# Four graph layers on one core: one pool of slabs from the first sweep through attention, and another order of the third sweep

## The chip, the cores and the metric

The kernel runs on one NeuronCore of a Trainium2 chip. Its engines are TensorE (PE, matrix products; PEld is its weight load), VectorE (DVE), ScalarE (ACT), GpSimd (POOL) and SyncE (SP, which here only issues transfers). The metric is the device time of one execution in microseconds, the median over several runs; lower is better. The time before is 1585.27 us, the median of 3 runs (1582.21 to 1586.68).

## The reference

There are 4096 nodes with 64 features, `x`, and one dense-stored 4096 x 4096 matrix `adj` of edge weights (0 or 0.05 to 0.06). Four layers follow one another, each with a residual sum and a layer norm over the features:

```python
x = _layernorm(x + _L0_gnn_ref(x, adj, ...))        # Chebyshev terms
x = _layernorm(x + _L1_gnn_ref(x, adj, adj, ...))   # graph attention and two GRU cells
x = _layernorm(x + _L2_gnn_ref(x, adj, ...))        # sum over neighbours, weights decaying with rank
x = _layernorm(x + _L3_gnn_ref(x, adj, ...))        # hyperbolic aggregation
```

Layer 0 is what most of the change touches: with `T0 = x`, `T1 = adj @ x`, `T2 = 2 adj @ T1 - T0`, `T3 = 2 adj @ T2 - T1`, the sum of `Tk @ W[k]` over k. Layer 1 needs, for every node, the features summed over the positive entries of its row (a product with the mask `adj > 0`), the same for the negative ones, softmax weights that depend only on the sign of an entry, and the product of the row with the features. Both signs are provided for; these inputs hold none below zero.

## The kernel before, in words

`adj` is cut into 8 x 8 slabs (g, c) of 512 x 512, 1 MB each: row group g (four blocks of 128 rows) and chunk c (four blocks of 128 columns). PE contracts over partitions, so a slab has to stand transposed; the kernel transposes all of `adj` once, keeps the transposed slabs `at` in a DRAM scratch `adj_t`, and reads them from there later.

**First sweep** (lines 525 to 577). For every g and for c from 7 down, SP loads a slab as `raw` (line 169, pool `rows0` with five buffers of 8 KB per partition), PE transposes its 16 blocks (line 536), ACT copies them out (line 543), POOL's queue writes the slab to `adj_t` (line 567), DVE reduces `raw` twice: row sums (line 569) and the lowest entry (line 571). Slabs with c >= g at once serve for `T1`, those with c < g for both `T1` and the part of `T2` that can be had already; each row group ends in `after_first`. Beside it run the loads and small preparations of weights (`aside`) and the transposes of `x` into `tr_a` (line 519, through `to_columns`, line 201). Six slabs stay in SBUF (`here`: (7,0) to (7,3), (6,6), (7,7)).

**Second sweep** (lines 617 to 626): the slabs with c > g, from g = 6 down, finish `T2`. A group ends in `after_second`: ACT copies the sum (line 447), PE brings it back to rows by products with the identity (line 467), DVE stores `T2` (line 600), PE multiplies by the layer's weights (line 457) and DVE adds that to `acc_t` (line 602).

**Third sweep** (lines 633 to 645): the slabs with c <= g give `T3`; group g has g + 1 slabs. The groups come in the order 7, 0, 1, 2, 3, 4, 5, 6. PE runs eight half-width products per slab (line 436). A group ends in `after_third`, put off by one slab (`Behind`): ACT copies the sum (line 447), PE forms the product with the weights plus `acc_t` times the identity (line 467, sixteen instructions), DVE adds `x` (line 608), norms, centres and splits into three bf16 parts (lines 230 to 261, 215 to 219). The normed rows are turned into `tr_a` (`turned_third`, line 614, through line 201) after the next group's slabs; the last group's turn is left to attention. Slabs are read back through `load0` (line 591) into the buffers of `rows0`.

**Attention** (`attention`, lines 870 to 977) goes through all 64 slabs again, g from 7 down, c from 0 up. It stands in a branch on whether any entry is negative; code inside a branch isn't mixed with code outside it. `masks` loads a slab (`load1`, line 660), DVE forms the mask `pos` (line 665), POOL's queue writes it to `mask_t` for layer 2 (line 669), and PE runs `wide` (line 906), `narrow` (line 914) and `weighed` (line 923), about 3.1 us in all. Masks are made two slabs ahead (`lead`). Steps of the previous group's end (`group_end`) follow one by one after slabs. The slabs' buffers are four of the pool `cols1`, and one in `front`, which is loaded and masked ahead of the branch. Near the end, and wherever the planner finds SP free, the first masks of layer 2 are loaded (`load2`, lines 680 to 683).

Layer 2 (lines 1052 to 1126) and layer 3 (from line 1143) follow.

**What sets the order.** Instructions are written in program order and a planner orders each engine's queue by its own estimate of when operands are there, earlier code first; `in_order` holds chosen instructions in their written order among themselves. [...] Buffers of a pool are given in rotation. Pools are laid out one after another; a pool opened after another was closed can take its place, and its first writers then wait for the last readers of what was there. `tri` (lines 123 to 135), a helper for the constant `follow`, is such a short-lived pool ahead of `rows0`.

Of the kernel before, what the change touches and what calls it, by code (L numbers as in the profile page):

```python
# [9 lines left out]
F32 = mybir.dt.float32  # L10
# [50 lines left out]
def gnn4_kernel(  # L61
# [21 lines left out]
    nc = tc.nc  # L83
# [14 lines left out]


# [60 lines left out]
    def gcols(g):  # L160
        return slice(g * GW, (g + 1) * GW)


    first_p = ctx.enter_context(ExitStack())
    rows_p = first_p.enter_context(tc.tile_pool(name="rows0", bufs=5))

    def load_raw(g, c):
        raw = rows_p.tile([P, GB, CB * P], F32, name="raw", tag="raw")
        nc.sync.dma_start(raw, adj[gcols(g), c * CB * P : (c + 1) * CB * P].rearrange("(b p) j -> p b j", p=P))
        return raw  # L170

    first_raw = [load_raw(0, NCH - 1)]
# [227 lines left out]


# [5 lines left out]
    with first_p, tc.tile_pool(name="acc", bufs=1) as acc_p, tc.tile_pool(name="win", bufs=1) as win_p, tc.tile_pool(  # L407
# [64 lines left out]
        dpart = sm.tile([P, NG, NCH, GB], F32, name="dpart")  # L472
        lows = sm.tile([P, NG * NCH], F32, name="lows")
# [122 lines left out]
        def after_second(g, ps):  # L596
            gs = gblocks(g)
            t_v = out_of(ps, "t_v")
            o = times(new_post(), [(t_v, ident[:, 0:F])])
# [4 lines left out]
        def after_third(g, ps):  # L604
            gs = gblocks(g)
            o = times(new_post(), [(out_of(ps, "t_h"), cheb[:, 3, :]), (acc_t[:, g // 2, :], ident[:, mine(g)])])
# [26 lines left out]
        done = []  # L633
        for n, g in enumerate([NG - 1] + list(range(NG - 1))):
            ps = ps_a.tile([P, GW], F32, name="pass3", tag=("h_ps", "w_ps")[n % 2])
            for c in reversed(range(g + 1)):
                at = load0(g, c)
                for k in range(CB):
                    halves(ps, 2, at[:, k, :], c * CB + k, c == g and k < 2, c == 0 and k >= CB - 2)
                later.flush()  # L640
            while done:
                turned_third(done.pop())
            later.push(lambda g=g, ps=ps: [after_third(g, ps), done.append(g)])
        later.flush()
        not_turned = done.pop()
# [12 lines left out]
    def load1(pool, g, c):  # L658
        at = pool.tile([P, CB, GW], F32, name="at1", tag="at")
        nc.sync.dma_start(at, adj_t[g][:, c * CB : (c + 1) * CB, :])  # L660
        return at

    def positives(pool, at):
        pos = pool.tile([P, CB, GW], MASK, name="pos")
        in_order(nc.vector.tensor_scalar(pos, at, 0.0, None, ALU.is_gt, saturate=False))  # L665
        return pos

# [19 lines left out]

# [5 lines left out]
    front = ctx.enter_context(ExitStack())  # L693
    front_p = front.enter_context(tc.tile_pool(name="front", bufs=1))
    with_at = [load1(front_p, NG - 1, c) for c in range(1)]
    with_pos = [positives(front_p, at) for at in with_at]


# [171 lines left out]
    def attention(signed, cols_p, sg, tl, ps_a, ps_p):  # L870
# [3 lines left out]
        def masks(g, c):  # L874
            if g == NG - 1 and c < len(with_at):
                at, pos = with_at[c], with_pos[c]
            else:
                at, pos = load1(cols_p, g, c), None
# [17 lines left out]
            up = sg.tile([P, CB, GW], F32, name="up")  # L896
# [34 lines left out]
        else:  # L931
# [5 lines left out]
        lead = 1 if signed else 2  # L937
        ahead = [masks(*order[n]) for n in range(lead)]
        steps = [
            lambda ps_p: to_columns(  # L940
                ps_p, tr_a[0 : F + 1, gcols(not_turned)], nat_a[:, gblocks(not_turned), :], F + 1, nc.scalar.copy
            )
        ]
# [36 lines left out]
    for signed in (True, False):  # L980
        with tc.If(any_negative > 0) if signed else cmp.Else() as block:
            cmp = block
            with tc.tile_pool(name="cols1", bufs=4 if not signed else 2) as cols_p, tc.tile_pool(name="sign1", bufs=2 if signed else 5) as sg, tc.tile_pool(
# [4 lines left out]
                attention(signed, cols_p, sg, tl, ps_a, ps_p)  # L988
# [521 lines left out]
```

## Time and profile before

| what | value |
|---|---|
| median of 3 runs | 1585.27 us (1582.21 to 1586.68) |
| the profiled execution | 1581.82 us, of which its span 1580.0 us |
| first sweep, from its first transposes | 18 to 374 us |
| second sweep | 376 to 488 us |
| third sweep, to attention's first product | 488 to 604 us |
| attention | 604 to 889 us |
| layers 2 and 3 | 889 to 1108, 1108 to 1580 us |
| busy share: PE, DVE, ACT, POOL | 90%, 74%, 52%, 6% |
| adj slabs, us from issue to landing (median) | `raw` 12.1, `at` 5.2 |

The page gives busy shares, the span in 40 slices with busy tenths, TensorE's granted clock and the load of the transfer engines, and groups of instructions by line. Answers of the trace give the waits (who waited, for whom, total us, times, longest), and the instructions of an engine in order of time, with start and length; in brackets stands the idle time before one and what ended it. In a list of stretches each line holds start and end, length, busy time of PE, PEld, DVE, ACT and POOL with the number of their instructions, granted clock, transfer share and GB/s. `SPq` is SP's own queue. Idle time of an engine that nobody waits for costs nothing.

### The profile page before, as it was taken

The page shows a single profiled execution, that of the slowest core. Times are in us where ns is not written, and L with a number is a line of the kernel's source. Part 1 is how long each engine was busy: PE and PEld are TensorE (multiplying, and loading weights), DVE is VectorE, ACT ScalarE, POOL GpSimd, SP SyncE. Part 2 cuts the span into 40 slices and gives each one's busy share as a digit, 9 for nine tenths or more (in the row PEclk, how much of TensorE's full clock was granted, in tenths as well). Part 3 has the DMA queues.
Part 4 walks back from the last instruction along what each step waited for, and adds up shares of the span by engine and source line. Part 5 has one row for each costly group of instructions (what it writes and reads, how often), then busy time and mean ns, then how long its engine had stood idle before and what let it go on. Part 6 is the DMA issues. An engine that isn't in the chain of part 4 may idle for free.

```text
span 1580.0 us, 19139 instructions
## 1 busy us (share of the span) xinstructions
PE 1418.8 (90%) x6851; PEld 691.3 (44%) x6874; DVE 1166.3 (74%) x2268; ACT 820.1 (52%) x1367; POOL 96.7 (6%) x162
## 2 busy tenths in 40 slices
PE   6899999999998987989999998789789999899995
PEld 4555555554443432333434444445333434344343
DVE  6788988982001534665676688888899999999997
ACT  3444444431000100222222588779888999898895
POOL 3001101000000001111111100000000000000000
PEclk9899999999999998999999999999899999999998
DMA  8999999996776778878978654442425444434430
GB/s 300 409 378 390 413 412 400 379 354 229 249 279 243 265 294 317 300 277 290 333 288 299 201 173 157 137 131 84 182 85 194 153 180 170 163 139 179 162 115 13
DMA packets 102336, 383.81 MB, mean 243 GB/s; under 512 B 15828, under 2 KB 16856, under 8 KB 70232
## 3 DMA queue, kind: packets, MB, share of 16 engines
q1 hardware_dynamic: 84256, 296.78, 52.9%
q0 software_dynamic: 14592, 84.16, 13.0%
q10 hardware_dynamic: 3384, 1.56, 0.5%
q8 instruction: 57, 0.93, 0.2%
q14 instruction: 47, 0.39, 0.1%
HBM read 297.26 MB, written 85.20 MB: 242 GB/s over the span
## 4 chain that ended last, share of the span: by engine, by line
PE 28%; DVE 22%; ACT 6%; DMA 2%; issue 2%; ACTq 0%; DVEq 0%; SPq 0%
PE v_ps L1227 6%; DVE wt L1103 5%; PE sums_ps L1287 4%; PE a_ps L923 3%; PE cnt_ps L1095 3%; DVE rt L1445 2%; DVE at_m L1273 2%; PE acc_ps L1064 2%; DMA at<-adj_t 2%; PE p_ps L906 2%; DVE f L1430 2%; PE post L729 1%; DVE at_d L1433 1%; DVE pos L665 1%; PE post L1271 1%
## 5 line engine op out<-in xcount | busy, mean ns | idle before, releaser
L543 ACT COPY at<-tp 128x512 f32<-128x512 f32 x256 | 133.0, 598 | 151.4 <-issue 106.2
L1101 ACT ACTIVATE wt<-cnt_ps 64x512 uint16<-64x512 f32 x288 | 163.1, 587 | 27.7 <-PE cnt_ps L1095 23.2
L1103 DVE TENSOR_SCALAR wt<-cnt_ps 64x512 uint16<-64x512 f32 x224 | 151.5, 692 | 29.6 <-PE cnt_ps L1095 23.8
L1227 PE MATMUL v_ps<-rv,tr_a 128*128 128x512 f32 (+1 forms) x288 | 142.2, 618 | 33.4 <-DVE rt L1445 32.5
L1095 PE MATMUL cnt_ps<-m,follow 128*64 128x512 fp8e4 x480 | 136.3, 390 | 23.1 <-DVE wt L1103 10.7
L569 DVE TENSOR_REDUCE dpart<-raw 128x4 f32<-128x2048 f32 x64 | 145.4, 2271 | 9.8 <-DMA raw<-in_adj_dram 9.8
L571 DVE TENSOR_REDUCE lows<-raw 128x1 f32<-128x2048 f32 x64 | 145.2, 2269 | 0.0
L536 PE MATMUL tp<-ident,raw 128*128 128x128 f32 x1024 | 133.7, 285 | 8.6 <-DMA raw<-in_adj_dram 8.6
L1287 PE MATMUL sums_ps<-at_d,nat_c 128*64 128x512 f32 x288 | 139.8, 606 | 1.4 <-DVE at_d L1433 1.0
L536 PEld LDWEIGHTS tp<-ident,raw 128*128 128x128 f32 x1024 | 117.2, 146 | 50.2 <-issue 41.2
L923 PE MATMUL a_ps<-at,nat_a 128*64 128x512 f32 x512 | 124.5, 613 | 2.9 <-DVE at L889 2.9
L665 DVE TENSOR_SCALAR pos<-at 128x2048 fp8e4<-128x2048 f32 x72 | 87.0, 1221 | 53.3 <-DMA at<-adj_t 43.4
L1292 PE MATMUL sums_ps<-at_m,nat_c 128*64 128x512 f32 x224 | 108.2, 605 | 0.0
L443 PE MATMUL w_ps<-at,cheb_n 128*128 128x512 f32 x224 | 101.1, 595 | 0.0
L443 PE MATMUL pass<-at,cheb_n 128*128 128x512 f32 x224 | 98.3, 596 | 0.7 <-DVE cheb_n L594 0.7
L1064 PE MATMUL acc_ps<-wt,sup_two 128*64 128x512 bf16 x512 | 96.6, 391 | 0.0
L1227 PEld LDWEIGHTS v_ps<-rv,tr_a 128*128 128x128 f32 x288 | 53.0, 199 | 83.9 <-DVE rt L1445 40.7
L1456 ACT ACTIVATE rt<-rt,one_col 128x1024 f32<-128x1024 f32 x72 | 78.7, 1094 | 17.4 <-DVE rt L1445 17.2
L1445 DVE SCALAR_TENSOR_TENSOR rt<-v_ps,rt 128x1024 f32<-128x1024 f32 x72 | 83.2, 1157 | 3.8 <-ACT rt L1421 3.6
L1430 DVE SCALAR_TENSOR_TENSOR f<-rt,w 128x1024 f32<-128x1024 f32 x72 | 82.8, 1158 | 3.3 <-ACT rt L1456 3.3
L1433 DVE TENSOR_TENSOR at_d<-at_d,f 128x1024 f32<-128x1024 f32 x72 | 83.2, 1156 | 0.1
L1273 DVE TENSOR_TENSOR at_m<-post,at_m 128x512 f32<-128x512 f32 x112 | 74.9, 683 | 9.6 <-PE post L1271 9.1
(346 smaller groups left out, 2262.3 us busy)
## 6 DMA issues: line engine op xcount, KB each, us to landing
at<-adj_t SPq DMA_DIRECT2D x122, 1024.0 KB, 5.2
raw<-in_adj_dram SPq DMA_DIRECT2D x64, 1024.0 KB, 12.1
adj_t<-at POOLq DMA_DIRECT2D x64, 1024.0 KB, 8.2
at_d<-adj_t SPq DMA_DIRECT2D x36, 1024.0 KB, 4.8
at_m<-adj_t SPq DMA_DIRECT2D x28, 1024.0 KB, 6.9
mask_t<-pos POOLq DMA_DIRECT2D x64, 256.0 KB, 6.1
m<-mask_t SPq DMA_DIRECT2D x120, 128.0 KB, 2.8
m<-mask_t SPq DMA_DIRECT2D x60, 256.0 KB, 4.1
```

What stands on the lines that cost most here:

```text
L443: in_order(nc.tensor.matmul(ps, lhsT=cheb_n[:, jb, k : k + 2, :], rhs=rhs, start=first, stop=last))
L536: in_order(nc.tensor.transpose(tp[:, cols(b)], raw[:, b, cols(k)], ident))
L543: nc.scalar.copy(at[:, k, :], tp)
L569: in_order(nc.vector.tensor_reduce(dpart[:, g, c, :], raw, AX.X, ALU.add))
L571: in_order(nc.vector.tensor_reduce(lows[:, n : n + 1], raw.rearrange("p b j -> p (b j)"), AX.X, ALU.min))
L923: in_order(nc.tensor.matmul(ps[q * F : (q + 1) * F, :], lhsT=nat_a[:, c * CB + k, 0:F], rhs=parts[q if signed else 0][:, k, :], start=(c = ...
L1064: in_order(nc.tensor.matmul(acc[a][q * F : (q + 1) * F, :], lhsT=parts[part], rhs=wt[2 * a + q].bitcast(BF16), start=(jb == NB - 1 and par ...
L1095: in_order(nc.tensor.matmul(cnt[q][mine, :], lhsT=follow, rhs=chunks[c][odd][q][:, k, :], start=(h == 2 * NB - 1), stop=True, skip_group_c ...
L1101: in_order(nc.scalar.activation(w, cnt[q][mine, :], AF.Relu, scale=-128.0))
L1103: in_order(nc.vector.tensor_scalar(w, cnt[q][mine, :], -128.0, 0.0, ALU.mult, ALU.max))
L1227: nc.tensor.matmul(vs[n][:, k, cs], lhsT=tr_a[:, cols(jb)], rhs=rights[i][0][:, cs], start=True, stop=True)
L1287: in_order(nc.tensor.matmul(bank[0:F, :], lhsT=nat_c[:, j * CB + k, :], rhs=own[t][:, k, :], start=(i == j and k == 0), stop=(j == seq[-1] ...
```

## The change

It has five parts.

- The pool of slabs `rows0`, and a small pool `front`, are laid out first, on the other side of SBUF, and stay until attention is over. The first slab's load stands first in the program.
- `attention` takes its slabs from `rows0` (five buffers) in place of its own pool `cols1` (four). `load1` and `positives` move up.
- The second sweep's ends go back to rows by transposes in place of products with the identity. The third sweep's ends are cut in three: `third_weighed` multiplies by the weights on the wide side and adds into `acc_t`; `after_third` transposes that, adds `x`, norms and splits; `turned_third` turns as before.
- The third sweep's groups come as 7, 0, 6, 1, 5, 2, 4, 3, and the three steps of an end are due one, two and six slabs after the group's last slab.
- After the last slab, four slabs for attention are asked for and the first mask is formed; then what is left of the ends runs, the last group's turn with it.

`dpart` and `lows` move to a pool that the first layer closes, and `up`, which only the signed branch uses, to another pool.

```diff
--- before.py
+++ after.py
@@ -96,6 +96,21 @@
     sm = ctx.enter_context(tc.tile_pool(name="sm", bufs=2))
     dram = ctx.enter_context(tc.tile_pool(name="dram", bufs=1, space=DRAM))
+    def gcols(g):
+        return slice(g * GW, (g + 1) * GW)
+    front = ctx.enter_context(ExitStack())
+    rows_p = front.enter_context(tc.tile_pool(name="rows0", bufs=5, side="right"))
+    front_p = front.enter_context(tc.tile_pool(name="front", bufs=1, side="right"))
+    def load_raw(g, c):
+        raw = rows_p.tile([P, GB, CB * P], F32, name="raw", tag="raw")
+        nc.sync.dma_start(raw, adj[gcols(g), c * CB * P : (c + 1) * CB * P].rearrange("(b p) j -> p b j", p=P))
+        return raw
+    first_raw = [load_raw(0, NCH - 1)]
     ident = const.tile([P, P], F32, name="ident")
     make_identity(nc, ident)
@@ -157,19 +172,6 @@
     mask_t = [dram.tile([P, NB + 1, GW], MASK, name=f"mask_t{g}") for g in range(NG)]
     none_t = const.tile([HP, GW], MASK, name="none_t")
-    def gcols(g):
-        return slice(g * GW, (g + 1) * GW)
-    first_p = ctx.enter_context(ExitStack())
-    rows_p = first_p.enter_context(tc.tile_pool(name="rows0", bufs=5))
-    def load_raw(g, c):
-        raw = rows_p.tile([P, GB, CB * P], F32, name="raw", tag="raw")
-        nc.sync.dma_start(raw, adj[gcols(g), c * CB * P : (c + 1) * CB * P].rearrange("(b p) j -> p b j", p=P))
-        return raw
-    first_raw = [load_raw(0, NCH - 1)]
     nc.scalar.dma_start(nat_a[:, :, 0:F], x.rearrange("(b p) f -> p b f", p=P))
     nc.gpsimd.memset(nat_a[:, :, F : F + 1], 1.0)
@@ -398,13 +400,23 @@
             lambda: state("hhe", whh_e), lambda: state("hhn", whh_n), turned_gat, gat_and_cell, score_weights,
         ]
-    with first_p, tc.tile_pool(name="acc", bufs=1) as acc_p, tc.tile_pool(name="win", bufs=1) as win_p, tc.tile_pool(
+    def load1(g, c):
+        at = rows_p.tile([P, CB, GW], F32, name="at1", tag="raw")
+        nc.sync.dma_start(at, adj_t[g][:, c * CB : (c + 1) * CB, :])
+        return at
+    def positives(pool, at):
+        pos = pool.tile([P, CB, GW], MASK, name="pos")
+        in_order(nc.vector.tensor_scalar(pos, at, 0.0, None, ALU.is_gt, saturate=False))
+        return pos
+    with tc.tile_pool(name="acc", bufs=1) as acc_p, tc.tile_pool(name="win", bufs=1) as win_p, tc.tile_pool(
         name="cols0", bufs=4
     ) as cols_p, tc.tile_pool(name="diag0", bufs=2) as diag_p, tc.tile_pool(
         name="ps_t0", bufs=3, space=PSUM
@@ -469,8 +481,8 @@
                     )
             return o
-        dpart = sm.tile([P, NG, NCH, GB], F32, name="dpart")
-        lows = sm.tile([P, NG * NCH], F32, name="lows")
+        dpart = acc_p.tile([P, NG, NCH, GB], F32, name="dpart")
+        lows = acc_p.tile([P, NG * NCH], F32, name="lows")
         later = Behind(1)
         put_off = []
@@ -596,14 +608,22 @@
         def after_second(g, ps):
             gs = gblocks(g)
             t_v = out_of(ps, "t_v")
-            o = times(new_post(), [(t_v, ident[:, 0:F])])
+            o = new_post()
+            for b in range(GB):
+                nc.tensor.transpose(o[:, b, :], t_v[0:F, cols(b)], ident[0:F, 0:F])
             nc.vector.scalar_tensor_tensor(cheb_n[:, gs, 2, :], o, 2.0, part[:, gs, :], ALU.mult, ALU.add)
             o, to = weigh(g, [(t_v, cheb_23)])
             nc.vector.tensor_tensor(to, o, to, ALU.add)
-        def after_third(g, ps):
+        def third_weighed(g, ps):
+            o, y_t = weigh(g, [(out_of(ps, "t_h"), cheb[:, 3, :])])
+            nc.vector.tensor_tensor(y_t, o, y_t, ALU.add)
+        def after_third(g):
             gs = gblocks(g)
-            o = times(new_post(), [(out_of(ps, "t_h"), cheb[:, 3, :]), (acc_t[:, g // 2, :], ident[:, mine(g)])])
+            o = new_post()
+            for b in range(GB):
+                nc.tensor.transpose(o[:, b, :], acc_t[mine(g), g // 2, cols(b)], ident[mine(g), mine(g)])
             y = sm.tile([P, GB, F], F32, name="y0", tag="y")
             nc.vector.tensor_tensor(y, o, nat_a[:, gs, 0:F], ALU.add)
             layernorm(nat_a[:, gs, 0:F], y)
@@ -630,19 +650,28 @@
                 deg[:, gblocks(g)], dpart[:, g, :, :].rearrange("p c b -> p b c"), AX.X, ALU.add
             )
-        done = []
-        for n, g in enumerate([NG - 1] + list(range(NG - 1))):
-            ps = ps_a.tile([P, GW], F32, name="pass3", tag=("h_ps", "w_ps")[n % 2])
+        due, n = [], 0
+        for m, g in enumerate(sum(([NG - 1 - i, i] for i in range(NG // 2)), [])):
+            ps = ps_a.tile([P, GW], F32, name="pass3", tag=("h_ps", "w_ps")[m % 2])
             for c in reversed(range(g + 1)):
                 at = load0(g, c)
                 for k in range(CB):
                     halves(ps, 2, at[:, k, :], c * CB + k, c == g and k < 2, c == 0 and k >= CB - 2)
                 later.flush()
-            while done:
-                turned_third(done.pop())
-            later.push(lambda g=g, ps=ps: [after_third(g, ps), done.append(g)])
-        later.flush()
-        not_turned = done.pop()
+                while due and due[0][0] <= n:
+                    due.pop(0)[2]()
+                n += 1
+            due += [
+                (n, m, lambda g=g, ps=ps: third_weighed(g, ps)), (n + 1, m, lambda g=g: after_third(g)),
+                (n + 5, m, lambda g=g: turned_third(g)),
+            ]
+            due.sort(key=lambda d: d[:2])
+        with_at = [load1(NG - 1, c) for c in range(4)]
+        with_pos = [positives(front_p, with_at[0])]
+        for work in due:
+            work[2]()
     three = ctx.enter_context(tc.tile_pool(name="three", bufs=1))
@@ -655,16 +684,6 @@
     sup_two = late.tile([P, NB, 2 * F], BF16, name="sup_two")
     sup_lo = late.tile([P, NB, F], BF16, name="sup_lo")
-    def load1(pool, g, c):
-        at = pool.tile([P, CB, GW], F32, name="at1", tag="at")
-        nc.sync.dma_start(at, adj_t[g][:, c * CB : (c + 1) * CB, :])
-        return at
-    def positives(pool, at):
-        pos = pool.tile([P, CB, GW], MASK, name="pos")
-        in_order(nc.vector.tensor_scalar(pos, at, 0.0, None, ALU.is_gt, saturate=False))
-        return pos
     def keep_mask(mask, g, c):
         nc.gpsimd.dma_start(mask_t[g][:, c * CB : (c + 1) * CB, :], mask)
@@ -684,16 +703,11 @@
         return to[QG:], to[:QG]
     last_p = [late.tile([P, GW], F32, name=f"last_p{q}") for q in range(2)]
     last_a = late.tile([P, GW], F32, name="last_a")
     wq = late.tile([P, 2, H3], F32, name="wq")
     first_masks = [late.tile([P, CB, GW], MASK, name=f"first_mask{n}") for n in range(2 * QG)]
-    front = ctx.enter_context(ExitStack())
-    front_p = front.enter_context(tc.tile_pool(name="front", bufs=1))
-    with_at = [load1(front_p, NG - 1, c) for c in range(1)]
-    with_pos = [positives(front_p, at) for at in with_at]
@@ -867,15 +881,15 @@
         return [lambda ps_p, part=part: [work(ps_p) for step in part for work in step] for part in parts]
-    def attention(signed, cols_p, sg, tl, ps_a, ps_p):
+    def attention(signed, sg, tl, ps_a, ps_p):
         Q = 2 if signed else 1
         def masks(g, c):
             if g == NG - 1 and c < len(with_at):
-                at, pos = with_at[c], with_pos[c]
+                at, pos = with_at[c], with_pos[c] if c < len(with_pos) else None
             else:
-                at, pos = load1(cols_p, g, c), None
+                at, pos = load1(g, c), None
             if not signed and pos is None:
                 pos = positives(sg, at)
             mask = pos
@@ -893,7 +907,7 @@
             if not signed:
                 return (pos,), (at,)
             neg = sg.tile([P, CB, GW], MASK, name="neg")
-            up = sg.tile([P, CB, GW], F32, name="up")
+            up = tl.tile([P, CB, GW], F32, name="up")
             in_order(nc.vector.tensor_scalar(neg, at, 0.0, None, ALU.is_lt, saturate=False))
             nc.scalar.activation(up, at, AF.Relu)
             in_order(nc.vector.tensor_scalar_min(at, at, 0.0))
@@ -934,13 +948,9 @@
             nc.gpsimd.memset(wq[:, 1, :], 0.0)
             nc.gpsimd.memset(last_p[1], 0.0)
         order = [(g, c) for g in reversed(range(NG)) for c in range(NCH)]
-        lead = 1 if signed else 2
+        lead = 0 if signed else 2
         ahead = [masks(*order[n]) for n in range(lead)]
-        steps = [
-            lambda ps_p: to_columns(
-                ps_p, tr_a[0 : F + 1, gcols(not_turned)], nat_a[:, gblocks(not_turned), :], F + 1, nc.scalar.copy
-            )
-        ]
+        steps = []
         for n, (g, c) in enumerate(order):
             if n + lead < len(order):
                 ahead.append(masks(*order[n + lead]))
@@ -980,12 +990,12 @@
     for signed in (True, False):
         with tc.If(any_negative > 0) if signed else cmp.Else() as block:
             cmp = block
-            with tc.tile_pool(name="cols1", bufs=4 if not signed else 2) as cols_p, tc.tile_pool(name="sign1", bufs=2 if signed else 5) as sg, tc.tile_pool(
+            with tc.tile_pool(name="sign1", bufs=2 if signed else 5) as sg, tc.tile_pool(
                 name="tail1", bufs=1
             ) as tl, tc.tile_pool(name="ps_a1", bufs=1 if signed else 2, space=PSUM) as ps_a, tc.tile_pool(
                 name="ps_p1", bufs=2, space=PSUM
             ) as ps_p:
-                attention(signed, cols_p, sg, tl, ps_a, ps_p)
+                attention(signed, sg, tl, ps_a, ps_p)
     front.close()
     nc.gpsimd.memset(tr_o, 0.0)
```

## The prediction

> **What bounds the kernel now.** I read the page's slices first, then the waits of SP, then busy time by stretch, then PE's waits and its order of time in the third sweep, and last SP's waits in attention. Slices of 39.5 us:
>
> ```profile
> span 1580.0 us, 19139 instructions
> ...
> PE   6899999999998987989999998789789999899995
> ...
> PEclk9899999999999998999999999999899999999998
> ```
>
> Up to slice 16 PE is at nine tenths except in slices 0 and 1 (to 79 us) and 12, 14 and 15 (474 to 513, 553 to 632 us); the clock digit falls in 1 and 15. The change touches just these places; the later dips lie in attention and layers it leaves alone. The stretches below give busy time by engine, clock and DMA share:
>
> ```profile
> 18.00:138.00 120.00, 108.72 (x618) 66.40 (x619) 102.41 (x89) 55.88 (x113) 11.73 (x22) 0.94 1.02 392
> 138.00:338.00 200.00, 200.00 (x1037) 118.24 (x1036) 176.21 (x134) 87.72 (x171) 19.66 (x37) 1.00 1.02 396
> 376.00:488.00 112.00, 111.54 (x290) 50.14 (x290) 6.68 (x12) 4.45 (x8) 0.00 (x0) 1.00 0.73 253
> 488.00:604.00 116.00, 93.61 (x454) 41.38 (x455) 48.99 (x203) 11.83 (x25) 0.72 (x2) 0.91 0.70 258
> 604.00:889.00 285.00, 261.75 (x1256) 109.68 (x1257) 178.19 (x511) 59.61 (x124) 46.98 (x65) 0.98 0.82 294
> ```
>
> The first sweep (18 to 374) has PE and DMA both full, the second (376 to 488) is PE alone, the third (488 to 604) is neither: PE idles 22 us there and its clock is 0.91. Why the first sweep starts at 18 is in SP's waits up to 18 us:
>
> ```profile
> SPq L169 <- DVE follow L135: 11.4, 1, 11.4
> ```
>
> The first slab of the adjacency is issued at 12.23, when DVE has last read the small `tri` tile: the buffers of `rows0` lie where `tri` was. PE's waits from 488 to 604, SP's from 480 to 604, and PE's order of time:
>
> ```profile
> PE post L201 <- DVE nat_a L261: 12.2, 5, 4.6
> PE post L467 <- ACT t_h L447: 2.2, 3, 0.7
> ```
> ```profile
> SPq L660 <- PE post L467: 12.8, 1, 12.8
> ```
> ```profile
> 513.51 3.68 PE L436 MATMUL pass<-at,cheb_n 128*64 128x512 f32 x8
> ...
> 519.25 1.94 PE L436 MATMUL pass<-at,cheb_n 128*64 128x512 f32 x8
> ...
> 604.10 1.86 PE L906 MATMUL p_ps<-pos,sp_two 128*128 128x512 fp8e4 x4 [7.77 <-DVE pos L665]
> ```
>
> The turn of a normed row (L201) waits for its norm while slabs stand ready behind it; after such a wait eight matmuls take 3.68 us, not 1.94. The first mask comes 7.77 us after the sweep's last matmul: its slab was not asked for until then (SP's 12.8), and DVE had the last norm first. In attention, PE waits only 8.3 us for masks after the first, and SP is held by loads of already written masks:
>
> ```profile
> SPq L680 <- DMA mask_t<-pos: 30.5, 4, 13.2
> ```
>
> **What the Trainium skill says.** "TensorE: Matmul & The Clock Gate", What's actually happening: about 3.4 us of idleness halve the clock, about 3.4 us of work restore it. The trace agrees (3.68 against 1.94), though 2.78 us of waiting sufficed at 524. "DMA: Bandwidth & Descriptors", Queues, rings and completion order: a DMA engine takes turns between queues by packet. No trace here shows x against slabs. "Perfetto Trace Analysis", Transposes: use a transpose rather than a plain matmul with the identity. The trace agrees: such a matmul of fp32 is two instructions (L467, eight for four blocks, 1.04 us), a transpose one (L201, four in 0.58).
>
> **The change part by part.**
>
> *Layout and first load.* On the right side `rows0` shares nothing with `tri`, so the load leaves at about 0.8 instead of 12.23: at most 11.4 us. Three things take from that. Now x (issued 0.86, landed 8.5, alone then) shares the engines; with two slabs of 2.6 us each (1 MB at 406 GB/s) between its packets it lands near 13. ACT issues fourteen small loads until 11.9 and loads its table, so its first copy is at 12.8, the first eviction of a slab (19.16 before) about 13. And 23 of the 32 transposes of x (0.16 each, 3.7 us of PE) ran inside the wait and now meet a full PE. Against that, PE's 8.6 us of waits for slabs between 18 and 100 mostly go, as DMA is ahead. I take 6.5: the 6 us by which evictions come earlier, the last two terms nearly cancelling; ends 3 and 11. PE never waits for a slab after 100 us, so what is won stays. `dpart` and `lows` only move: nothing.
>
> *Second sweep's ends* turn by transposes: eight instructions at 1.04 us become four at about 0.52. PE is full, so 7 x 0.5 = 3.5 us (0.5 of it beside the third sweep's start). Ends 2 and 4.
>
> *Third sweep.* Before, 488.3 to 604.1 is 115.8 us: 36 slabs x 1.71 = 61.6; the last end of the second sweep 1.9; eight ends of sixteen L467 instructions, 2.13 each, 17.0; seven turns x 0.58 = 4.1; waits 12.2 + 2.2 + 0.7; the last 7.8. These make 107.5; the 8.3 left are the half clock.
> After: 61.6 + 1.9 + eight ends of weighing (two L457 instructions, 0.87), four transposes (0.52) and a turn (0.58), 15.8: 79.3. (The 0.5 above is already counted with the second sweep.) Work of a row's end is now due one, two and six slabs after it, and a long row follows each short one. From y to the centred row DVE needs 4.5 us (596.4 to 600.8), with its splits 6.2. The turn, at least four slabs (6.8 us) after its norm starts, is covered. What is late next is the sum in `acc_t`: it stands on DVE behind the neighbour row's norm, and the transposes wait for it. For rows 0, 1 and 2 the distance falls short by about 4.6, 2.9 and 1.2 us; a half clock follows the first two, some 4 us. Where DVE takes the sum in its gap for ACT's root, most of this goes. The planner may also advance an end, as at 565.92 now (2.78 us). I take 10 us for all; ends 3 and 20.
> Slabs: 30 less five loaded ahead, and the first of attention, 26 x 2.6 = 68 us, under PE's 79: not the bound, but close.
>
> *Seam.* Four slabs of attention are issued on SP in the sweep, ahead of the branch, each when PE frees a buffer; attention's later loads queue behind. The first mask (1.22 us of DVE) stands ahead of the last row's sum and norm. That adds a wait: should its slab be late, sum, norm and both turns of row 3 wait on DVE and PE. The slab lands about one slab time behind the sweep's last, so I count 1.9 us. The last turn, formerly behind attention's first slab, now stands before the branch and waits for the norm. So PE loses ACT's copy 0.75, 1.9, and the norm 4.7: 7.4 us, hardly less than the 7.8 of before.
> After in all: 79.3 + 10 + 7.4 = 96.7, a gain of 19; ends 7 and 27.
>
> *Attention.* Four buffers of `cols1` and one used once become five in rotation: one more slab (3.1 us of PE work) of lead while masks block SP. Of the 8.3 us of waits for masks I take 2; ends -4 and 6, as the planner orders the same loads anew. `up` concerns the signed branch, not run. PE's work, mask writes on POOL and the later stages stay.
>
> *Sum:* 6.5 + 3.5 + 19 + 2 = 31. The profiled execution took 1581.8 (span 1580.0 and 1.8 around it), 3.5 below the median of 1585.3. The gain leaves 1549 of the span, and 1554 of the median.
>
> **Rivals.**
> *Small gain:* the planner puts row ends ahead of slabs that are in fact there, and x starves behind five slabs at the start. For it: L201 stalls after three slabs of row 5 show that the planner's slabs come later than real ones. Against: the ends' work is shorter and due later. 3 + 3 + 8 + 1 = 15: 1570. That the layout does not free the first load belongs here too; it costs the 6.5.
> *Large gain:* no half clock inside the sweep and DMA's head start fully used: 11 + 3.5 + 26 + 4 = 44: 1541. For it: PE's eight slab waits and clock drops at 43, 64 and 108 us lie in the first sweep's start. Against: DMA share 1.02 and ACT's issuing.
> *Slower:* mask loads placed early on SP hold all slabs of attention behind them, now that SP is ahead. Four such blocks exist, the longest 13.2 us. Five buffers cover 5 x 3.1 = 15.5 us; losing the 31 gained and 5 more over four groups needs blocks of 15.5 + 9 = 24.5 us each. From there it decides; at 30 us, 4 x 14.5 = 58 lost: 1612. Against: a mask written is 6.1 us away from its landing, and the extra slab is the very cover.
>
> **How the numbers follow.** Forecast 0.55 (own range 1546 to 1563), small 0.22, large 0.14, slower 0.05; no change 0.04. The range, 1541 to 1575, cuts part of the outer cases. 0.3% (4.8 us) is about what a measurement of this kernel tells from no change. Faster 0.91, same 0.04, slower 0.05.
>
> **What would show it.** First slab issued before 2 us, first eviction near 13, second sweep begun 6 us earlier; half as many instructions in the second sweep's turns; no L201 wait over 1 us inside the third sweep, but waits of transposes on DVE's `acc_t`; attention's first matmul near 575 (604 - 6.5 - 3.5 - 19); the first mask's DVE instruction before the last norm. I am wrong if the first evictions stay at 19, if the third sweep waits on slabs, or if attention takes longer than its 285 us.

## The result

The changed kernel takes 1923.2 us (median of four, 1922.2 to 1923.6), the kernel before, timed beside it, 1583.8 (1582.2 to 1586.7). The ratio is 1.2139, with a 95% interval of 1.2118 to 1.2161: slower by 21%, where the forecast was 1554 and faster.

From here on, line numbers are those of the changed kernel, and "attention" is the stretch from its first to its last `wide` product (L920; L906 before). The expectations below count it to the end of its last products, some 3 us longer (284 where the table here has 281.1). The page of the changed kernel, with its head, slices of 48 us, the row of the mask instruction and the row of the slab load:

```profile
span 1920.5 us, 18940 instructions
...
PE   6999999999976646555555556798798899999995
...
PEclk9999999999997777777676767899898999999998
...
L410 DVE TENSOR_SCALAR pos<-at 128x2048 fp8e4<-128x2048 f32 x72 | 87.9, 1225 | 317.0 <-DMA at<-adj_t 316.6
...
at<-adj_t SPq DMA_DIRECT2D x122, 1024.0 KB, 4.8
```

From slice 12 (576 us onwards, counted from 0) to slice 25 PE falls to between four and seven tenths, and the digit of its clock to six or seven but for the last. The mask instruction's own work is what it was (87.9 us in 72), but DVE sat idle 317.0 us ahead of it, nearly all of that for slabs; before, 53.3, of which 43.4 for slabs:

```profile
L665 DVE TENSOR_SCALAR pos<-at 128x2048 fp8e4<-128x2048 f32 x72 | 87.0, 1221 | 53.3 <-DMA at<-adj_t 43.4
```

A slab takes 4.8 us from issue to landing. The stretches (columns: length, busy time of PE, PE's weight loads, DVE, ACT and POOL, granted clock, DMA share, GB/s):

```profile
18.00:138.00 120.00, 110.24 (x651) 65.97 (x652) 111.09 (x114) 62.85 (x126) 18.85 (x34) 0.99 1.00 391
...
370.00:482.00 112.00, 110.08 (x276) 46.77 (x276) 8.11 (x16) 4.46 (x8) 0.00 (x0) 1.00 0.73 253
482.00:578.00 96.00, 80.94 (x375) 29.31 (x376) 52.50 (x211) 12.47 (x26) 1.69 (x3) 0.97 0.87 343
578.00:1230.00 652.00, 378.68 (x1262) 133.83 (x1261) 185.60 (x514) 61.10 (x126) 38.78 (x64) 0.74 0.36 124
```

The third sweep with its seam is down from 116 to 96 us, as forecast, and the DMA share in it up from 0.70 to 0.87. Attention is where the time went: 652 us for what took 285, at a DMA share of 0.36 and a clock of 0.74.

Stage by stage, each boundary being the start of a product:

| stretch | before | after | difference |
|---|---|---|---|
| start and first sweep, to the second sweep's first product | 376.0 | 372.7 | -3.3 |
| second sweep | 112.3 | 109.6 | -2.7 |
| third sweep and seam, to attention's first product | 115.8 | 95.5 | -20.3 |
| attention, first to last `wide` product | 281.1 | 645.4 | +364.3 |
| the rest of the span | 694.8 | 697.3 | +2.5 |
| span | 1580.0 | 1920.5 | +340.5 |

What attention waits for is in SP's waits of the whole run (line, releaser, us in total, times, longest):

```profile
SPq L405 <- DVE pos L410: 312.3, 55, 18.6
...
SPq L405 <- PE a_ps L937: 226.2, 55, 12.0
...
SPq L699 <- DMA mask_t<-pos: 42.7, 5, 8.6
```

The loads of slabs wait 55 times for the mask of a slab and 55 times for its `weighed` product, both of them readers of the buffer that the load wants. The loads of written masks, the mechanism of my slower rival, wait 42.7 us in all, 8.6 at most: not that. In order of time, attention looks like this in its middle (start, duration, engine, line, and in brackets the idle time ahead and what ended it):

```profile
801.61 18.62 SPq L405 DMA_DIRECT2D at<-adj_t  x3
...
806.48 1.23 DVE L410 TENSOR_SCALAR pos<-at 128x2048 fp8e4<-128x2048 f32 x1 [11.13 <-DMA at<-adj_t]
807.76 1.87 PE L920 MATMUL p_ps<-pos,sp_two 128*128 128x512 fp8e4 x4 [6.19 <-DVE pos L410]
...
809.56 1.06 PE L928 MATMUL p_ps<-pos,sp_lo 128*64 128x512 fp8e4 x4
...
810.41 2.35 PE L937 MATMUL a_ps<-at,nat_a 128*64 128x512 f32 x8
...
817.61 1.23 DVE L410 TENSOR_SCALAR pos<-at 128x2048 fp8e4<-128x2048 f32 x1
```

A load goes out at 801.61, and 4.87 us later its mask begins. PE, idle for 6.19 us, multiplies from 807.76 to 812.8. The next mask comes at 817.61, again one load after the last of those products. (SP's row runs together three issues that lie within 18.62 us.) Load, mask and products, which should overlap, follow each other: one buffer is in use.

The code has five. Four of them are filled by `with_at = [load1(NG - 1, c) for c in range(4)]` (L671), ahead of the branch. A buffer filled there and read inside the branch is not given back inside it: with 64 slabs to load, four buffers serve one slab each, and the fifth serves the other 60. The start of attention shows it (SP's queue, DVE's masks, PE's `weighed` products):

```profile
565.03 0.33 SPq L405 DMA_DIRECT2D at<-adj_t  x1
```
```profile
596.00 0.32 SPq L405 DMA_DIRECT2D at<-adj_t  x1
```
```profile
579.35 4.64 DVE L410 TENSOR_SCALAR pos<-at 128x2048 fp8e4<-128x2048 f32 x4
```
```profile
587.82 3.60 PE L937 MATMUL a_ps<-at,nat_a 128*64 128x512 f32 x16
...
594.07 1.88 PE L937 MATMUL a_ps<-at,nat_a 128*64 128x512 f32 x8
```

The fifth slab's load goes out at 565.03. All five masks are formed by 584.0 and the products of the first four slabs are over by 591.4, yet the sixth load leaves only at 596.00, when the fifth slab's products end. The four buffers that had been read are not used again. That is the theory that the runs below test: **held buffers**. PE's waits in attention, in the changed kernel and then before:

```profile
PE p_ps L920 <- DVE pos L410: 139.1, 29, 8.6
PE a_ps L937 <- DMA at<-adj_t: 56.1, 13, 4.9
PE p_ps L928 <- DVE pos L410: 52.9, 8, 8.7
PE a_ps L937 <- DVE at L903: 14.6, 3, 7.0
```
```profile
PE p_ps L906 <- DVE pos L665: 9.8, 2, 7.8
...
PE p_ps L914 <- DVE pos L665: 6.3, 7, 1.4
PE a_ps L923 <- DVE at L889: 2.9, 1, 2.9
```

On PE the price has two parts. Waits for slabs and masks are 262.7 us, where they were 11.2 (the 7.8 ahead of the first product belongs to the seam), so 251 us more. And the same products run at the lower clock, 376.0 us of busy time where they took 261.2. The two parts make 366, close to the 364 of the table.

### The profile page after: what moved, and what is told of

It is laid out like the page before. It is cut to its first block, busy times and chain, and to the rows that moved or that the text cites. A ratio compares the mean times of both kernels' runs of the same rounds, so it can differ in the third digit from the quotient of the medians.

```text
span 1920.5 us, 18940 instructions
## 1 busy us (share of the span) xinstructions
PE 1518.2 (79%) x6766; PEld 694.6 (36%) x6766; DVE 1175.1 (61%) x2276; ACT 819.6 (43%) x1367; POOL 89.8 (5%) x162
## 4 chain that ended last, share of the span: by engine, by line
PE 54%; DVE 21%; DMA 17%; ACT 5%; issue 2%; DVEq 0%; ACTq 0%; SPq 0%
DMA at<-adj_t 12%; PE a_ps L937 9%; PE pass L455 5%; PE v_ps L1237 5%; PE w_ps L455 5%; PE tp L548 4%; DVE wt L1113 4%; PE p_ps L920 4%; DMA raw<-in_adj_dram 4%; PE sums_ps L1297 4%; DVE pos L410 3%; PE pass L448 3%; PE cnt_ps L1105 2%; PE p_ps L928 2%; DVE rt L1455 2%
## 5 line engine op out<-in xcount | busy, mean ns | idle before, releaser
L410 DVE TENSOR_SCALAR pos<-at 128x2048 fp8e4<-128x2048 f32 x72 | 87.9, 1225 | 317.0 <-DMA at<-adj_t 316.6
L937 PE MATMUL a_ps<-at,nat_a 128*64 128x512 f32 x512 | 181.7, 849 | 70.8 <-DMA at<-adj_t 56.1
L920 PE MATMUL p_ps<-pos,sp_two 128*128 128x512 fp8e4 x256 | 100.2, 535 | 142.4 <-DVE pos L410 139.1
L548 PE MATMUL tp<-ident,raw 128*128 128x128 f32 x1024 | 132.6, 283 | 16.8 <-DMA raw<-in_adj_dram 12.7
L980 ACT COPY p_t<-p_ps 128x512 f32<-128x512 f32 x7 | 4.1, 585 | 304.8 <-PE p_ps L920 304.8
L937 PEld LDWEIGHTS a_ps<-at,nat_a 128*64 128x64 f32 x512 | 49.7, 196 | 168.5 <-issue 83.1
L928 PE MATMUL p_ps<-pos,sp_lo 128*64 128x512 fp8e4 x256 | 62.4, 579 | 52.9 <-DVE pos L410 52.9
L920 PEld LDWEIGHTS <-sp_two 128*128 128x128 bf16 x256 | 27.2, 117 | 209.0 <-issue 202.4
```

The costliest lines, as they stand in the source:

```text
L548: in_order(nc.tensor.transpose(tp[:, cols(b)], raw[:, b, cols(k)], ident))
L920: in_order(nc.tensor.matmul(ps[q], lhsT=sp_two[:, jb, :], rhs=two[q][:, k, :], start=(jb == 0), stop=(jb == NB - 1)))
L937: in_order(nc.tensor.matmul(ps[q * F : (q + 1) * F, :], lhsT=nat_a[:, c * CB + k, 0:F], rhs=parts[q if signed else 0][:, k, :], start=(c = ...
```

## The experiments

The rivals: **the queue**, in which the four slabs issued ahead of the branch, or the loads of written masks, hold up SP; and **the branch itself**, whose entry costs time whatever was loaded.

### No branch

The two arms become one; the signed attention and the test are left out.

```diff
-    for signed in (True, False):
-        with tc.If(any_negative > 0) if signed else cmp.Else() as block:
+    for signed in (False,):
+        if True:
```

> The changed kernel without the branch: only the attention for entries without a negative sign is there, the signed one and the test of the sign are left out (these inputs need neither). Four slabs are still asked for ahead and all share five buffers. Theory 'held' (a buffer filled ahead of the branch is given back only when the branch ends, so four of five are lost inside it): without a branch they come back one by one, attention takes 275 to 290 us as before the change, in all about 1550 (1540 to 1562). Rival 'shared' (the shared pool, or the four loads ahead on SP's queue, make each load wait for its forerunner's mask and products whatever stands around): attention stays near 650 us, in all about 1920.

Measured: 1545.3 us, ratio 0.9734 (0.9691 to 0.9777). Four slabs are still asked for ahead, on the same queue. Its stretch of attention and its seam in PE's order of time:

```profile
574.00:854.00 280.00, 261.38 (x1256) 109.42 (x1256) 176.73 (x514) 59.79 (x123) 50.37 (x63) 0.98 0.80 287
```
```profile
573.76 1.09 PE L203 MATMUL post<-ident,nat_a 128*65 128x128 f32 x4 [6.51 <-DVE nat_a L263]
574.64 1.91 PE L920 MATMUL p_ps<-pos,sp_two 128*128 128x512 fp8e4 x4
```

Attention is back at a clock of 0.98 and takes 275.7 us, 5.4 less than before the change. Whether the fifth buffer brings that is not shown: PE's waits for masks are 7.1 us where they were 8.3, and the branch is gone too. But the queue is not the cause of the loss; holding inside the branch is. The run takes out the block and the signed arm, which reads the same slabs, together: whether the end of the block or the other arm's reads keeps the buffers was not told apart.

### One, two and three slabs ahead

```diff
-        with_at = [load1(NG - 1, c) for c in range(4)]
+        with_at = [load1(NG - 1, c) for c in range(1)]
```

and likewise with 2 and with 3.

> The changed kernel with one slab asked for ahead of the branch in place of four. 'Held': one buffer is lost, four rotate as in the kernel before; attention 280 to 292 us, in all 1557 (1548 to 1567). 'Shared': about 1920.

Measured with one ahead: 1556.0 us, ratio 0.9798 (0.9755 to 0.9841). Attention takes 278.1 us.

> The changed kernel with two slabs ahead of the branch, so three of five buffers rotate inside it. Held buffers: a mask is made two slabs ahead of its products and its slab is kept until the second of them, so three buffers are just what that lead needs; attention then takes 281 us as with one ahead, up to 300 where a load comes late, and the time is 1556 to 1575 (ratio 0.980 to 0.993). If every held buffer cost something, attention would lie near the middle between one ahead (281) and three ahead (369), about 325, and the time near 1600 (ratio 1.009).

Measured with two: 1582.1 us, ratio 0.9976 (0.9959 to 0.9992). Attention takes 307.4 us, and misses both expectations: three buffers nearly do, but not quite. Its profile shows where the time goes (PE's and DVE's waits in this run, then PE's before the change):

```profile
PE post L831 <- DVE n L763: 19.4, 6, 5.4
```
```profile
DVE pos L410 <- DMA at<-adj_t: 70.9, 26, 10.7
```
```profile
PE post L817 <- DVE n L749: 9.2, 6, 2.7
```

PE waits little more for masks (12.7 us against 8.3). It waits longer for `n`, a tile of the previous group's end (19.4 us against 9.2): DVE forms masks between these steps, and idles for their slabs (70.9 us against 43.4). PE's products take some 10 us more, at a clock of 0.94.

> Three slabs ahead. 'Held': two buffers rotate. A slab's round in one buffer is about 10.2 us in the changed kernel (650 us for 64), so two give 5.1 to 5.6 us per slab where PE alone needs 4.4: attention 325 to 350, in all 1600 (1590 to 1625). 'Shared': about 1920.

Measured with three: 1647.4 us, ratio 1.0373 (1.0315 to 1.0430). Attention takes 366.0 us. The direction is right; the size is missed upwards, and the profile says by what. Its attention, and PE's waits there:

```profile
583.00:953.00 370.00, 283.90 (x1252) 113.35 (x1253) 181.15 (x511) 58.40 (x122) 38.39 (x64) 0.91 0.62 218
```
```profile
PE p_ps L920 <- DVE pos L410: 70.0, 22, 5.9
...
PE p_ps L928 <- DVE pos L410: 2.0, 3, 1.3
```

Waits for masks are 72.0 us, 64 more than before the change. PE's busy time is 283.9 us against 261.8: 22 us more for the same products, at a clock of 0.91 instead of 0.98. I had counted the waits and left out that slower products follow many of them: after 13 of the 21 waits of more than 2.4 us for a mask, products at half speed come next (0.63 us each in place of 0.38), after the other 8 none come in the next 4 us. The two together make 86, and attention grew by 84.9.

### One and two buffers in the kernel before

Here nothing is moved; `cols1` is made smaller. The first slab lies in `front`, outside the rotation, as it does before.

```diff
-            with tc.tile_pool(name="cols1", bufs=4 if not signed else 2) as cols_p, ...
+            with tc.tile_pool(name="cols1", bufs=1 if not signed else 2) as cols_p, ...
```

and likewise with 2.

> The kernel before, its attention's own pool cut from four buffers to one; nothing else changed, no pool is shared and one slab is loaded ahead as before. 'Held' (one rotating buffer is the whole cost): attention about 650 us where it took 285, in all about 1945 (1915 to 1975). 'Shared': it has nothing to share; then the loss in the changed kernel is not one of buffers alone and this run stays below 1800.

Measured with one: 1971.4 us, as expected, ratio 1.2413 (1.2338 to 1.2488). SP's waits in it:

```profile
SPq L660 <- DVE pos L665: 304.4, 58, 10.2
SPq L660 <- PE a_ps L923: 227.3, 58, 6.3
```

The pair of waits of the changed kernel, and nearly its size (58 times each), in a kernel without a line of the change. Per slab that rotates the price is the same: (665.0 - 281.1) / 63 = 6.1 us here, and (645.4 - 275.7) / 60 = 6.2 in the changed kernel, against its version without the branch.

> The kernel before with two buffers of cols1 where it has four, and nothing else. If three ahead was dear in the changed kernel only through the two buffers left, attention takes about 369 us here too, where it took 284, less some 3 us for the extra slab that the kernel before holds outside its rotation: time 1655 to 1675 (ratio 1.045 to 1.057). If the blocking of the sweep's own queue by the slabs ahead is part of it, attention takes 325 to 350 here: time 1625 to 1650.

Measured with two: 1687.9 us, ratio 1.0636 (1.0586 to 1.0686). Attention takes 387.5 us, above what either theory said. It is 21 us longer than with three ahead in the changed kernel; that one has three slabs in hand when attention starts and this one a single slab, but no run shows that this makes all of the 21. What the run was to tell, it tells: two buffers alone cost this much, without any slab of attention asked for in the sweep.

All of these in one view:

| buffers that rotate in attention | kernel | attention, us | clock there | PE's waits for masks and slabs in it, us |
|---|---|---|---|---|
| 1 | changed (4 held) | 645.4 | 0.74 | 262.7 |
| 1 | before, `cols1` of 1 | 665.0 | 0.74 | 282.3 |
| 2 | changed, 3 ahead | 366.0 | 0.91 | 72.0 |
| 2 | before, `cols1` of 2 | 387.5 | 0.87 | 80.0 |
| 3 | changed, 2 ahead | 307.4 | 0.94 | 15.6 |
| 4 | changed, 1 ahead | 278.1 | 0.98 | 10.1 |
| 4 | before | 281.1 | 0.98 | 11.2 |
| 5 | changed, no branch | 275.7 | 0.98 | 10.0 |

The wait ahead of attention's first product is left out. The other versions below that rotate four take 277.6 to 282.0 us, so the 275.7 of five is 2 us under the lowest of them; no run tells the fifth buffer from the missing branch.

### The layout and the first load alone

The kernel before, with only `rows0` on the right side and the first slab asked for ahead of the constants.

```diff
+    rows_p = first_p.enter_context(tc.tile_pool(name="rows0", bufs=5, side="right"))
...
+    first_raw = [load_raw(0, NCH - 1)]
+
     ident = const.tile([P, P], F32, name="ident")
...
-    rows_p = first_p.enter_context(tc.tile_pool(name="rows0", bufs=5))
...
-    first_raw = [load_raw(0, NCH - 1)]
```

> The kernel before with the first part of the change alone: the five buffers of the slabs are laid out first, on the other side, and the first slab's load stands first; they are closed after the first layer as before, and attention is as before. The forecast gave this part 6.5 us (3 to 11). By the changed kernel's profile I now expect less: there x landed at 16.2 us, not 13, ACT was busy issuing small loads until 19.9, not 11.9, and its first eviction came at 21.2, later than the 19.2 of before; the second sweep begins 3.3 us earlier. So 2 to 4 us, 0.998 (0.994 to 1.001). If the head start is used after all: 0.993 or less.

Measured: 1576.5 us, ratio 0.9945 (0.9924 to 0.9966). That is a gain of 5 to 12 us; the forecast had 6.5, while the profiles of before and after show 3.3 (second sweep begun at 376.0 and 372.7; in this run at 372.5). Which is true? Kernels that are alike up to the second sweep begin it at different times. Before, and its versions with one and two buffers: 376.0, 383.2, 381.1, mean 380.1. The changed kernel and six versions with the same start (no branch; one, two, three ahead; the two under "The ends' order"): 372.7, 371.9, 372.3, 371.0, 378.7, 371.4, 376.2, mean 373.5. The difference is 6.6 us, though the two groups overlap. The profile of before happened to be an early one.

The way to it is not the forecast's. ACT's queue, SP's and PE's start in the changed kernel:

```profile
1.80 10.00 ACTq L277 DMA_DIRECT2D cheb<-in_L_gnn_weight_dram  x2
...
21.16 1.56 ACT L555 COPY at<-tp 128x512 f32<-128x512 f32 x3
```
```profile
0.81 25.75 SPq L109 DMA_DIRECT2D raw<-in_adj_dram  x6
```
```profile
16.20 1.54 PE L203 MATMUL post<-ident,nat_a 128*65 128x128 f32 x6 [6.67 <-DMA nat_a<-in_x_dram]
...
26.73 1.94 PE L448 MATMUL h_ps<-at,cheb_n 128*64 128x512 f32 x8
```

The first slab leaves at 0.81 as forecast. But ACT is held 10.00 us by two loads that took it 4.51 before, PE can start on x only at 16.20, where the forecast had x landed near 13, and the first eviction of a slab begins at 21.16 and not at 13. It was 19.16 before, so the first steps are later, and the first product of the sweep too (26.73 against 24.46). What is won comes after that. Of PE's waits for slabs between 30 and 370 us the three runs with the old start show 7.5, 9.3 and 9.1 us, the seven with the new one 2.8 to 7.0, mean 4.8; and the clock between 18 and 138 us is 0.93 or 0.94 in the former, 0.94 to 1.00 in the latter, mean 0.98. That is 3.8 us less waiting and, over 120 us, an estimated 5 us of clock; the 2 us or so that the first product is late go off. This adds up, but no run takes the two apart.

### The small loads out of the way

One slab ahead of the branch; x and the first weights go out on SP before the first slab, the other weights on POOL's queue.

```diff
+    nc.sync.dma_start(nat_a[:, :, 0:F], x.rearrange("(b p) f -> p b f", p=P))
...
+        nc.sync.dma_start(cheb[q * F : (q + 1) * F, :, :], w_cheb.rearrange("k i o -> i k o"))
...
-        nc.scalar.dma_start(wh, w_hyp)
+        nc.gpsimd.dma_start(wh, w_hyp)
```

> One slab ahead, and at the start x and the first layer's weights go on SP's queue ahead of the first slab, the other small loads on POOL's queue, none on ACT's. If x starved behind the slabs and ACT held by its issues ate the head start: x lands near 8, the first slab near 11, first eviction near 12 where it was 21, second sweep begun 5 to 9 us sooner than 372, in all 1549 (1544 to 1554), ratio 0.975. If the first sweep is bound by transfers from start to end, whoever comes first: 1555, ratio 0.979.

Measured: 1554.1 us, ratio 0.9805 (0.9772 to 0.9838); one ahead alone had 0.9798. PE's order of time, and its waits from 30 to 370 us:

```profile
9.13 1.94 PE L206 MATMUL post<-ident,nat_a 128*65 128x128 f32 x8 [9.13 <-DMA nat_a<-in_x_dram]
...
19.51 1.94 PE L448 MATMUL h_ps<-at,cheb_n 128*64 128x512 f32 x8
```
```profile
PE tp L548 <- DMA raw<-in_adj_dram: 10.6, 6, 6.4
```

The sweep's first product comes at 19.51, 6 us earlier than with one ahead alone (25.52). But the slabs start at 6.75 instead of 0.81, and PE then, from 30 us on, waits 10.6 us for them where one ahead alone has 5.4. The second sweep begins at 368.5, earlier than in any run that leaves these loads where they were; the time doesn't follow. Attention is longer in this profile (280.8 us against 278.1), which takes part of it back; whether that is more than scatter is open. No gain is shown.

### The ends' order, and the last turn

With one slab ahead, the third sweep's rows in the order of before (7, 0, 1 ... 6), all else kept:

```diff
-        for m, g in enumerate(sum(([NG - 1 - i, i] for i in range(NG // 2)), [])):
+        for m, g in enumerate([NG - 1] + list(range(NG - 1))):
```

> One slab ahead, the third sweep's groups again in the order 7, 0, 1, ..., 6, its ends still cut in three and due one, two and six slabs later. If it is the long and short rows in turn that keep PE from waiting for DVE, the short rows' ends pile up on DVE again: third sweep 6 to 10 us longer than with the new order (95 to 96 us from its first product to attention's), ratio 0.985. If the cut ends and their distance do it, at most 3 us longer: 0.980.

Measured: 1558.4 us, ratio 0.9829 (0.9799 to 0.9859), between the two. From the third sweep's first product to attention's it takes 98.9 us, with the new order 95.7 (one ahead), before the change 115.8. PE's waits in it, and with the new order:

```profile
PE post L203 <- DVE nat_a L263: 9.6, 4, 4.5
```
```profile
PE post L203 <- DVE nat_a L263: 7.5, 3, 5.4
```

The order is worth some 3 of the 20 us, by the profile; the others are left for the transposes in place of products, the later due times and the early mask, which no run takes apart. The times of the two kernels lie too close to confirm the 3.

Second, with one slab ahead and the new order, the last row's turn put back into attention's steps:

```diff
-        for work in due:
+        for work in due[:-1]:
             work[2]()
+        not_turned = NG // 2 - 1
...
-        steps = []
+        steps = [
+            lambda ps_p: to_columns(
+                ps_p, tr_a[0 : F + 1, gcols(not_turned)], nat_a[:, gblocks(not_turned), :], F + 1, nc.scalar.copy
+            )
+        ]
```

> One slab ahead (as in the run with one), and the last group's turn is again a step behind attention's first slab, inside the branch. If PE's 5.4 us of waiting for the last norm ahead of the branch is on the path, attention's first product comes 5 to 7 us sooner after the sweep (about 8 us after its last slab's products, where it was 13) and the whole is 1550 (1546 to 1555), ratio 0.976. If the first mask or the branch itself sets that time, nothing moves: 0.980.

Measured: 1547.2 us, ratio 0.9766 (0.9734 to 0.9799): as expected. The seam on PE, of the changed kernel and then of this one:

```profile
573.43 1.08 PE L203 MATMUL post<-ident,nat_a 128*65 128x128 f32 x4 [5.38 <-DVE nat_a L263]
577.83 1.89 PE L920 MATMUL p_ps<-pos,sp_two 128*128 128x512 fp8e4 x4 [3.31 <-issue]
```
```profile
573.02 1.87 PE L921 MATMUL p_ps<-pos,sp_two 128*128 128x512 fp8e4 x4 [6.24 <-DVE sp_rest L218]
```

In the changed kernel PE waits 5.38 us for the norm, turns, and then stands 3.31 us for nothing that the profile shows. I put this down to the entry of the branch: in the six profiles that have the turn ahead of the branch it is 2.9 to 3.4 us, and in the run without a branch it is missing. With the turn inside, PE enters the branch while the norm is still on DVE, and the two overlap. The third sweep and seam come down from 95.7 to 92.0 us.

Last, both together, the turn inside and the small loads out of the way.

> One slab ahead, the last turn back inside the branch, x and the first Chebyshev weights asked for on SP ahead of the first slab, the other small weights on the queue of POOL. The turn alone measured 0.9766 of the kernel before; the start alone showed a second sweep that began 3.8 us earlier in its profile, and nothing in its ratio. If that gain is real: 0.9745 (0.971 to 0.977). If it is lost again: 0.9766 (0.974 to 0.979).

Measured: 1552.9 us, ratio 0.9795 (0.9763 to 0.9827): not better than the turn alone; the moved loads are worth nothing that can be measured. The best version of the whole computation is the one with one slab ahead and the last turn inside, 2.3% under the kernel before and 19.6% under the changed one (1547.2 against 1923.2; the two were not timed side by side).

## Why the prediction was wrong

**The step that failed** is the attention's: "Four buffers of `cols1` and one used once become five in rotation". They do not become five in rotation; four are held and one rotates. From this sentence I took a gain of 2 us, ends -4 and 6, and it was a loss of 364. What the step needed was in the text ahead of it: code inside the branch is not mixed with code outside, and the one slab that the kernel before loads ahead has a buffer of its own, which nobody asks back. I counted four slabs issued early as four slabs gained, and did not ask when each buffer is given back. Of the signs of being wrong, "if attention takes longer than its 285 us" came true by far. "If the first evictions stay at 19" did too: they came at 21.16, later than before.

**The slower rival** ended on the right side by a mechanism that did not happen: the loads of written masks hold SP 8.6 us at the longest, under the 15.5 at which it was to begin.

**The other terms held in size, two of them partly by luck.** With one slab ahead, which leaves four buffers to rotate as before the change and keeps the rest, the gain by the ratio is 25 to 39 us, 32 in the middle; the forecast without attention's 2 was 29.

- *Start, 6.5:* right as a sum (6.6 between the means of ten profiles, 5 to 12 by the times), wrong on its way, so luck. "The first eviction of a slab about 13" was 21.16, and "ACT issues fourteen small loads until 11.9" (there are thirteen) became 19.8. The gain is in fewer waits later in the sweep, which I had set off against the late turns of x, and in the clock, which stood only in the large rival.
- *Second sweep's ends, 3.5*, of which 3.0 lie inside it: 2.7.
- *Third sweep and seam, 96.7:* measured 95.5. Two misses nearly cancel, which is luck. The seam's waits are 0.74 + 0.21 + 5.38 + 3.31 = 9.6, not 7.4, since the entry of the branch was left out. What lies over the 79.3 inside the sweep is 95.5 - 79.3 - 9.6 = 6.6, not 10: the transposes wait for `acc_t` 0.79 us and not "4.6, 2.9 and 1.2", and no half clock follows; instead a turn waits 1.7 for its norm, where I had none over 1.
- *Attention with five rotating:* where they do rotate, without the branch, 5.4 us less, inside -4 to 6. The 2 us were to come out of PE's waits for masks, and these fell by 1.2; what the rest comes from is open.

The chances were wrong for the same reason as the number: none of the cases had a buffer that stays taken.

## What to carry over

When a load moves to an earlier place, ask of its buffer when it comes back, and not only when it is filled: here a slab loaded ahead of a branch took its buffer out of the rotation for the whole of the branch, so prefetch only as many as the loop inside can spare, or give them buffers of their own. Count the buffers left against the lead of the loop; here masks run two slabs ahead, four rotating buffers sufficed, three cost 29 us of attention, two 88 and one 367. And set the last wait ahead of a branch where its entry can run under it.

## What the runs showed of the hardware

- Starving PE costs twice. With 53 waits for slabs and masks, 5 us each on average and 8.7 at most, the same products took 376 us of PE's time and not 261, at a granted clock of 0.74.
- A slab asked for alone takes 4.8 us from issue to landing, while the 406 GB/s that all transfers together reached from 218 to 258 us of the kernel before would bring 1 MB in an estimated 2.6. With one buffer that latency is paid for each slab.
- PE stands 2.9 to 3.4 us at the branch where no wait covers it (3.31 in the changed kernel, and five others beside it), and not at all in the run without a branch.
- Two strided loads that ACT issues in 4.5 to 4.7 us as long as no slab is under way (three profiles) held it for 9.5 to 10.2 us beside slabs on SP's queue (eight profiles).
